# Softmax transposes by VectorE blocks and DRAM, f_j by a DRAM broadcast, two moved gate products and a greater hop in the plan of a four-layer graph network

## The chip, the cores and the metric

The kernel runs on one core of a Trainium2 chip. The metric is the device time in microseconds (us) of one execution. The engines are TensorE (PE), VectorE (DVE), ScalarE (ACT), GpSimd (POOL) and SyncE (SP); here SP issues all the DMAs.

## The reference

There are 128 graphs of 128 nodes with 256 features, and an integer adjacency matrix for each. Four layers follow one another. Each ends with a residual and a normalisation over the features.

```python
# layer 0: four edge scores, chosen by the value of adj
s_k   = leaky_relu(einsum('bid,bjd->bij', x * a_k, x), 0.2)
alpha = softmax(where(adj == k + 1, s_k, NEG_INF))
x = layernorm(x + alpha @ x)
# layer 1: mean of the messages over the incoming edges
msg = einsum('bij,biu->bju', adj, x @ W_msg)
deg = sum(adj, axis=1)
x = layernorm(x + relu(x @ W_upd + msg / max(deg, 1) + bias))
# layer 2: three steps of a gated recurrent unit (GRU)
for i in range(3):
    aggr = einsum('bst,bsd->btd', adj != 0, h @ weight[i])
    h = gru_cell(aggr, h, w_ih, w_hh, b_ih, b_hh)
x = layernorm(x + h)
# layer 3: additive attention
Wh  = x @ W
f_i, f_j = Wh @ a1, Wh @ a2
e   = leaky_relu(f_i[:, :, None] + f_j[:, None, :], 0.2)
alpha = softmax(where(adj > 0, e, NEG_INF))
x = layernorm(x + elu(alpha @ Wh))
```

## The kernel before, in words

Four graphs make a group (G = 4), so that a tile of 128 partitions by 512 columns holds one feature half of a whole group. There are 32 groups (NG = 32). All is float32.

The program is not written in the order in which it runs. The functions `loading`, `layer0`, `layer1`, `gru` and `layer3` only record operations, with their engine, an estimated duration and their dependencies. At the end a planner walks through modelled time. At each step it takes the engine that can start first. Among that engine's operations that are ready by then it takes the one with the least nominal time, and issues it for good. So each engine's order is fixed when the kernel is built, and on the chip an engine runs its list in that order, each instruction as soon as its inputs are there.

The nominal times come from `paced`: a group's GRU fills one period of 91 us, its layer 0 lies two periods to one ahead of that, its layer 1 less than one period ahead, and its layer 3 in the period after. So PE finds products of the layers 0, 1 and 3 of other groups to do while the GRU's chain waits on its other engines. The operations of the GRU are "urgent": on the engines other than PE they go ahead of all others. A result is taken as ready `HOP` (0.3 us) after its producer's end for an urgent consumer, and `SLACK` (1.0 us) after for another. A DMA takes 0.6 us of SP and lands `LANDING` (2.6 us) later.

Three ways of turning and spreading data matter here.

A PE transpose against `ident` goes to a PSUM bank and is copied out by ACT. The function `softmax` does it for the probabilities: four transposes in one bank, then the copy to `probT`. It serves layer 0 and layer 3. In `layer3` PE also spreads f_j, which is column 1 of `wh`, over the partitions: it transposes that column broadcast to 128 columns, and `leaky` reads the result from PSUM into the tile `e`.

The functions `turned` and `back` turn without PE. `DVE.transpose` turns each 32x32 block within its place into a tile `z_...`, one DMA writes it to a DRAM tile `way_...`, and four DMAs fetch the blocks to where they belong. This serves the output of layer 0 (tags 1: z_1, x1T), the output of layer 1 (z_2, h0T) and the new hidden state of each GRU step (z_h, hn). The number of buffers of `z` is 2 where the tile has four blocks of columns (z_2 and z_h), 1 for z_1.

A GRU step's function `step` records the products of the old state with `w_hhT` (`of_h`, in two halves 0 and 1 of the features) and those of the aggregated messages `agT` with `c_gi` (`of_m`), gate by gate: reset R, update Z and candidate C, two halves each. The R and Z gates have PSUM banks of their own (`gate`), the others use `ps`, four banks that all the layers share. `aggregate` multiplies the turned state `hn` by the adjacency, and ACT copies the result to `agT`. `update` makes the new state `hT` on DVE, after which it is turned again.

A float32 product of 128 rows with 512 columns appears as two matmul records in the trace, a PE transpose of 128x128 as one.

Of the kernel before, what the change touches and what calls it, by code (L numbers as in the profile page):

```python
# [17 lines left out]
def kernel(  # L18
# [36 lines left out]
    P = 128  # L55
# [30 lines left out]
    class View:  # L86
# [23 lines left out]
        def to_broadcast(self, shape):  # L110
            return View(self.buf, shape, self.box, self.steps + (("to_broadcast", (shape,), {}),))

        def real(self):
            ap = self.buf.memory()
            for name, a, k in self.steps:
                ap = getattr(ap, name)(*a, **k)
            return ap

    def tile_of(tag, shape, bufs=1, dtype=F32, pool=work):
        buf = Buf(pool, list(shape), dtype, tag, bufs)  # L120
        return View(buf, list(shape), [(0, n) for n in shape])
# [79 lines left out]
                )  # L201


    LANDING = 2.6
    HOP = 0.3
    SLACK = 1.0

    def pe_cost(op, n, sums):
# [151 lines left out]

    def turned(src, n, tag):

        z = tile_of(f"z_{tag}", [P, n, P], 2 if n == 4 else 1)
        DVE.transpose(z, src)
        way = tile_of(f"way_{tag}", [n, P, P], 4, F32, dram)
        SP.dma_start(out=way.rearrange("n p c -> p n c"), in_=z)
        return way
# [31 lines left out]
                res[:, b, :], res[:, b, :], AF.Identity, bias=nmr[:, b : b + 1], scale=rstd[:, b : b + 1]  # L399
            )  # L400

    def softmax(alpha, tag):

        nmax = tile_of(f"nmax_{tag}", [P, G], 2)
        DVE.tensor_reduce(nmax, alpha, AX.X, OP.max, negate=True)
        p = tile_of(f"prob_{tag}", [P, G, N])
        rs = tile_of(f"rsum_{tag}", [P, G], 2)
        for b in range(G):
            ACT.activation(
                p[:, b, :], alpha[:, b, :], AF.Exp, bias=nmax[:, b : b + 1], scale=1.0,  # L410
                accum_out=rs[:, b : b + 1],
            )
        rinv = tile_of(f"rinv_{tag}", [P, G], 2)
        DVE.reciprocal(rinv, rs)
        ps = bank()
        with PE:
            for b in range(G):
                PE.transpose(ps[:, b * N : (b + 1) * N], p[:, b, :], ident)
        pT = tile_of(f"probT_{tag}", [P, G, N])
        ACT.copy(pT, ps.rearrange("p (b n) -> p b n", b=G))  # L420
        return pT, rinv

    def leaky(out, in_, bias):
# [20 lines left out]
    def layer0(g, s):  # L444

        s.a_f = a_f = tile_of("a_f", [P, G, N], 2)
        POOL.tensor_copy(a_f, s.adj)
        alpha = tile_of("alpha0", [P, G, N])
        POOL.memset(alpha, NEG0 / SLOPE)
        xT = []  # L450
        for c in range(KC):
            t = tile_of("xT", [P, T], 3)
            DVE.transpose(t, s.x_blocks[:, c].rearrange("p i f -> p (i f)"))
            xT.append(t)


        def prepared(k):
            mk = tile_of("mk", [P, G, N], 3, U8)
            DVE.tensor_scalar(mk, a_f, float(k + 1), None, op0=OP.is_equal)
            xs = []  # L460
            for c in range(KC):
                t = tile_of("xs", [P, T], 4)
                if c == 0:
                    POOL.tensor_scalar(t, xT[c], acol[:, k, c : c + 1], None, op0=OP.mult)
                else:
                    ACT.mul(t, xT[c], acol[:, k, c : c + 1])
                xs.append(t)
            return mk, xs

        ready = [prepared(0)]  # L470
        for k in range(4):
            if k < 3:
                ready.append(prepared(k + 1))
            mk, xs = ready.pop(0)
            ps = bank()
            with PE:
                PE.needs(mk)
                for b in range(G):
                    cols = slice(b * N, (b + 1) * N)
                    for c in range(KC):  # L480
                        PE.matmul(ps[:, cols], xT[c][:, cols], xs[c][:, cols], start=(c == 0), stop=(c == KC - 1))
            DVE.copy_predicated(alpha.rearrange(FLAT), mk.rearrange(FLAT), ps)

        leaky(alpha, alpha, 0.0)
        pT, rinv = softmax(alpha, "0")
        s.x1 = res = tile_of("xa", [P, G, D], 2)
        for h in range(G // 2):
            ps = bank()
            with PE:
                for j in range(2):  # L490
                    b = 2 * h + j
                    PE.matmul(ps[:, j * D : (j + 1) * D], pT[:, b, :], s.x[:, b, :], start=True, stop=True)
            for j in range(2):
                b = 2 * h + j
                DVE.scalar_tensor_tensor(
                    res[:, b, :], ps[:, j * D : (j + 1) * D], rinv[:, b : b + 1], s.x[:, b, :],
                    op0=OP.mult, op1=OP.add,
                )
        normalise(res, *statistics(res, "0"), "0")
        way = turned(res.rearrange("p b (c n) -> p (b c) n", c=KC), G * KC, "1")  # L500
        s.x1T = tile_of("x1T", [P, G, KC, N])
        back(s.x1T.rearrange("p b c n -> p (b c n)"), way)
# [44 lines left out]
    def gru(g, s):  # L547
# [5 lines left out]
        def step(i, hT, hn):  # L553
# [63 lines left out]
            q1 = hidden(1, terms(C + 1, of_h=both, start=True, stop=True))  # L617
            terms(R, of_h=[1])
            terms(R + 1, of_h=[1])
            terms(Z, of_h=[1])  # L620
            terms(Z + 1, of_h=[1])
            for c in range(KC):
                aggregate(c)
            t0 = reset(0, terms(R, of_m=both, stop=True), q0)
            t1 = reset(1, terms(R + 1, of_m=both, stop=True), q1)
            n0, d0 = candidate(0, terms(C, of_m=both, start=True, stop=True), t0)
# [10 lines left out]
    def layer3(g, s):  # L637


        rT = []  # L640
        for c in range(KC):
            t = tile_of("rT", [P, T], 2)
            POOL.tensor_add(t, s.hT[c], s.h0T[c])
            rT.append(t)
        x3 = tile_of("xc", [P, G, D])
        for c in range(KC):
            cols = slice(c * P, (c + 1) * P)
            DVE.tensor_add(x3[:, :, cols], s.hn[c], s.x2[:, :, cols])
        mv, rstd = statistics(x3, "2")
        wh = tile_of("wh", [P, G, 2 + D])  # L650
        for b in range(G):
            ps = bank()
            with PE:
                for c in range(KC):
                    PE.matmul(
                        ps[:, : 2 + D], rT[c][:, b * N : (b + 1) * N], w3x[:, c, :],
                        start=(c == 0), stop=(c == KC - 1),
                    )
            ACT.mul(wh[:, b, :], ps[:, : 2 + D], rstd[:, b : b + 1])

        ps = bank()
        with PE:
            for b in range(G):
                PE.transpose(
                    ps[:, b * N : (b + 1) * N], wh[:, b, 1:2].to_broadcast([P, N]), ident
                )
        alpha = tile_of("alpha3", [P, G, N])
        POOL.memset(alpha, NEG3)
        e = tile_of("e", [P, G, N])
        for b in range(G):  # L670
            leaky(e[:, b, :], ps[:, b * N : (b + 1) * N], wh[:, b, 0:1])
        DVE.copy_predicated(alpha.rearrange(FLAT), s.m_gt.rearrange(FLAT), e.rearrange(FLAT))
        pT, rinv = softmax(alpha, "3")
        normalise(x3, mv, rstd, "2")

        res = tile_of("xd", [P, G, D], 2)
        neg = tile_of("neg", [P, G, D])
        for h in range(G // 2):
            ps = bank()
            with PE:  # L680
                for j in range(2):
                    b = 2 * h + j
                    PE.matmul(ps[:, j * D : (j + 1) * D], pT[:, b, :], wh[:, b, 2:], start=True, stop=True)
            for j in range(2):
                b = 2 * h + j
                pb = ps[:, j * D : (j + 1) * D]
                DVE.tensor_scalar(
                    neg[:, b, :], pb, rinv[:, b : b + 1], 0.0, op0=OP.mult, op1=OP.min
                )
                ACT.activation(res[:, b, :], pb, AF.Relu, scale=rinv[:, b : b + 1])  # L690
        for h in range(G // 2):
            half = slice(2 * h, 2 * h + 2)
            ACT.activation(neg[:, half], neg[:, half], AF.Exp)
            POOL.tensor_add(res[:, half], res[:, half], x3[:, half])
            DVE.scalar_tensor_tensor(res[:, half], neg[:, half], -1.0, res[:, half], op0=OP.add, op1=OP.add)
        normalise(res, *statistics(res, "3"), "3")
        SP.dma_start(out=out[g * G : (g + 1) * G].rearrange("b n d -> n b d"), in_=res)
# [69 lines left out]
    while left:  # L767
# [24 lines left out]
            buf.free_at = max(buf.free_at, end)  # L792
        for other in op.after.values():
            other.waiting -= 1
            hop = 0.0 if other.engine is e and not op.landing else HOP if other.urgent else SLACK
            other.ready = max(other.ready, end + hop)
            if other.waiting == 0:
                other.engine.ready.append(other)
# [29 lines left out]
```

## Time and profile before

| What | Value |
|---|---|
| Median of 3 runs | 3052.71 us (3050.05 to 3054.14) |
| Profiled execution | 3051.68 us |
| Its span, first to last instruction | 3049.9 us |
| PE busy | 2964.1 us, 97% of the span |
| DVE busy | 1918.7 us, 63% |
| ACT busy | 1234.7 us, 40% |
| POOL busy | 815.4 us, 27% |
| Mean granted PE clock | 0.991 |
| DMA: share of 16 engines, bytes | 35.1%, 232.27 MB |

A busy time is the union of an engine's records, so records that overlap in the pipeline count once. Every operation goes through one recording helper, so all carry the same line (L198) and are told apart by the names of their tiles. The names in the profile lack their numbers: `prob`, `probT` and `alpha` stand for both layer 0 and layer 3. In a row of the groups the columns are count, busy time and mean duration of one (ns), then the idle time of the engine just before, and what ended it. In a timeline row they are start and length in us, the engine, the operation, how many were merged, and in brackets an idle time before it.

### The profile page before, as it was taken

How to read it: one execution, taken by the hardware profiler on the slowest of the kernel's cores; microseconds unless marked ns; L12 is line 12 of the kernel's file. 1: busy time of each engine (PE TensorE's matmuls, PEld its weight loads, DVE VectorE, ACT ScalarE, POOL GpSimd, SP SyncE). 2: the span in 40 equal slices, each digit the busy share in tenths (PEclk: the TensorE clock that was granted, in tenths of full speed). 3: DMA queues.
4: the chain of work that ended last, by engine and by line, in shares of the span. 5: the costliest groups of instructions: out<-in, count | busy, mean ns of one | idle time of the engine just before them, and what ended most of it. 6: DMA issues, size and time to landing. Idle time of an engine off the chain costs nothing.

```text
span 3049.9 us, 33115 instructions
## 1 busy us (share of the span) xinstructions
PE 2964.1 (97%) x10456; PEld 1677.0 (55%) x10456; DVE 1918.7 (63%) x4315; ACT 1234.7 (40%) x2543; POOL 815.4 (27%) x711
## 2 busy tenths in 40 slices
PE   7899999999999999999999999999999999999996
PEld 5455555555555555555555555555555555555543
DVE  5556666566666566666566666666666566665644
ACT  2234444434444434443434444344444344434333
POOL 3222332222222222222223322222322222222222
PEclk9999999999999999999999999999999999999997
DMA  5333333233333333432333432343332344322321
GB/s 133 72 65 86 80 85 76 58 80 85 85 80 66 66 83 83 90 79 60 73 83 80 91 76 58 76 86 82 83 71 59 83 87 87 76 55 50 76 62 42
DMA packets 1034478, 232.27 MB, mean 76 GB/s; under 512 B 817984, under 2 KB 1034176, under 8 KB 1034304
## 3 DMA queue, kind: packets, MB, share of 16 engines
q1 hardware_dynamic: 1034304, 230.16, 35.1%
q8 instruction: 84, 1.38, 0.2%
q14 instruction: 90, 0.74, 0.1%
HBM read 129.38 MB, written 100.66 MB: 75 GB/s over the span
## 4 chain that ended last, share of the span: by engine, by line
PE 91%; DVE 4%; issue 1%; ACT 0%; POOL 0%; SPq 0%; DMA 0%; POOLq 0%; ACTq 0%
PE ps L198 50%; PE gate L198 41%; DVE hT L198 2%; DVE t_d L198 2%; DVE t_r L198 1%; DVE neg L198 0%; SPq L198 0%; ACT xd L198 0%; DVE z L198 0%; DVE xd L198 0%; DMA hn<-way_h 0%; POOL t_d L198 0%; ACT wh L198 0%; DVE st L198 0%; DVE z_h L198 0%
## 5 line engine op out<-in xcount | busy, mean ns | idle before, releaser
L198 PE MATMUL gate<-agT,c_gi 128*128 128x512 f32 x1536 | 711.0, 592 | 0.0
L198 PE MATMUL gate<-hT,w_hhT 128*128 128x512 f32 x1024 | 473.6, 595 | 26.6 <-DVE hT L198 26.6
L198 PEld LDWEIGHTS gate<-agT,c_gi 128*128 128x128 f32 x1536 | 286.8, 190 | 324.3 <-issue 321.0
L198 PE MATMUL ps<-agT,c_gi 128*128 128x512 f32 x768 | 360.7, 592 | 0.0
L198 PEld LDWEIGHTS gate<-hT,w_hhT 128*128 128x128 f32 x1024 | 191.9, 190 | 223.6 <-issue 170.0
L198 POOL TENSOR_TENSOR rstd<-rstd,neg_half 128x4 f32<-128x4 f32 x128 | 141.9, 1109 | 629.2 <-DVE rstd L198 604.8
L198 POOL TENSOR_SCALAR xs<-xT,acol 128x512 f32<-128x512 f32 x128 | 204.0, 1594 | 396.4 <-PE ps L198 389.9
L198 POOL TENSOR_TENSOR t_d<-hT,t_n 128x512 f32<-128x512 f32 x128 | 176.9, 1382 | 471.2 <-ACT t_n L198 467.5
L198 DVE SCALAR_TENSOR_TENSOR t_d<-t_z,t_d 128x512 f32<-128x512 f32 x192 | 196.2, 1022 | 140.6 <-POOL t_d L198 77.7
L198 DVE SCALAR_TENSOR_TENSOR t_r<-t_r,q 128x512 f32<-128x512 f32 x192 | 141.5, 737 | 224.9 <-ACT t_r L198 222.1
L198 ACT ACTIVATE q<-ps,bhn 128x512 f32<-128x512 f32 x192 | 132.0, 688 | 362.9 <-PE ps L198 362.9
L198 PEld LDWEIGHTS ps<-xs,xT 128*128 128x128 f32 x2048 | 243.4, 193 | 17.8 <-issue 15.9
L198 PE MATMUL ps<-xs,xT 128*128 128x128 f32 x2048 | 246.7, 276 | 0.3 <-DVE xb L198 0.3
L198 PE MATMUL ps<-hT,w_hhT 128*128 128x512 f32 x512 | 240.3, 593 | 4.3 <-DVE hT L198 4.3
L198 PE MATMUL ps<-w_um,x1T 128*128 128x512 f32 x512 | 241.5, 595 | 1.6 <-DMA x1T<-way 1.6
L198 ACT ACTIVATE t_n<-t_r,bih 128x512 f32<-128x512 f32 x192 | 138.3, 720 | 245.8 <-DVE t_r L198 245.8
L198 ACT COPY agT<-ps 128x512 f32<-128x512 f32 x192 | 112.5, 586 | 303.0 <-PE ps L198 303.0
L198 PE MATMUL gate<-h0T,w_hhT 128*128 128x512 f32 x512 | 235.0, 592 | 0.0
L198 ACT ACTIVATE t_r<-gate,brz 128x512 f32<-128x512 f32 x192 | 131.9, 687 | 253.5 <-PE gate L198 253.5
L198 PEld LDWEIGHTS ps<-agT,c_gi 128*128 128x128 f32 x768 | 145.7, 190 | 157.4 <-issue 154.0
L198 DVE TENSOR_TENSOR t_r<-t_r,ps 128x512 f32<-128x512 f32 x192 | 131.5, 685 | 145.0 <-PE ps L198 144.9
L198 POOL TENSOR_TENSOR t_d<-h0T,t_n 128x512 f32<-128x512 f32 x64 | 82.1, 1283 | 386.8 <-ACT t_n L198 386.8
(107 smaller groups left out, 4189.5 us busy)
## 6 DMA issues: line engine op xcount, KB each, us to landing
way_h<-z_h SPq DMA_DIRECT2D x192, 256.0 KB, 2.3
hn<-way_h SPq DMA_DIRECT2D x768, 64.0 KB, 2.5
x_blocks<-in_x_dram SPq DMA_DIRECT2D x256, 64.0 KB, 2.4
x_in<-in_x_dram SPq DMA_DIRECT2D x32, 512.0 KB, 4.1
way<-z SPq DMA_DIRECT2D x32, 512.0 KB, 4.3
x1T<-way SPq DMA_DIRECT2D x128, 128.0 KB, 3.0
way<-z SPq DMA_DIRECT2D x64, 256.0 KB, 2.6
h0T<-way SPq DMA_DIRECT2D x256, 64.0 KB, 2.5
```

Of the source, the lines that this page charges most:

```text
L198: getattr(self.engine, name)(*[a.real() if isinstance(a, View) else a for a in args], **{k: a.real() if isinstance(a, View) else a for k, ...
```

## The change

The softmax of layer 0 turns its probabilities with PE for the first group only, the softmax of layer 3 for the last group only. All the others use `turned` and `back` with the new tag p. For all groups but the last, f_j is written as a row per graph to DRAM, and read back with a broadcast to the 128 partitions, into the tile `fj`, on which `leaky` then works in place; the tile `e` is gone. `turned` keeps two buffers only for the tag h, so z_2 and z_p have one. In the GRU step the second halves of the update gates' `of_h` products are recorded behind the aggregates. In the planner, an urgent consumer on PE is taken as ready `PE_HOP` (0.7 us) after its producer.

```diff
+    PE_HOP = 0.7
...
     def turned(src, n, tag):
-        z = tile_of(f"z_{tag}", [P, n, P], 2 if n == 4 else 1)
+        z = tile_of(f"z_{tag}", [P, n, P], 2 if tag == "h" else 1)
...
-    def softmax(alpha, tag):
+    def softmax(alpha, tag, quick):
...
-        ps = bank()
-        with PE:
-            for b in range(G):
-                PE.transpose(ps[:, b * N : (b + 1) * N], p[:, b, :], ident)
         pT = tile_of(f"probT_{tag}", [P, G, N])
-        ACT.copy(pT, ps.rearrange("p (b n) -> p b n", b=G))
+        if quick:
+            ps = bank()
+            with PE:
+                for b in range(G):
+                    PE.transpose(ps[:, b * N : (b + 1) * N], p[:, b, :], ident)
+            ACT.copy(pT.rearrange(FLAT), ps)
+        else:
+            back(pT.rearrange(FLAT), turned(p, G, "p"))
         return pT, rinv
...
-        pT, rinv = softmax(alpha, "0")
+        pT, rinv = softmax(alpha, "0", g == 0)
...
             terms(R + 1, of_h=[1])
+            for c in range(KC):
+                aggregate(c)
             terms(Z, of_h=[1])
             terms(Z + 1, of_h=[1])
-            for c in range(KC):
-                aggregate(c)
...
-        ps = bank()
-        with PE:
-            for b in range(G):
-                PE.transpose(
-                    ps[:, b * N : (b + 1) * N], wh[:, b, 1:2].to_broadcast([P, N]), ident
-                )
+        fj = tile_of("fj", [P, G, N])
+        if g < NG - 1:
+            way = tile_of("way_f", [G, N], 4, F32, dram)
+            SP.dma_start(out=way.rearrange("b n -> n b"), in_=wh[:, :, 1])
+            SP.dma_start(out=fj, in_=way.partition_broadcast(P))
+            rows = [fj[:, b, :] for b in range(G)]
+        else:
+            ps = bank()
+            with PE:
+                for b in range(G):
+                    PE.transpose(ps[:, b * N : (b + 1) * N], wh[:, b, 1:2].to_broadcast([P, N]), ident)
+            rows = [ps[:, b * N : (b + 1) * N] for b in range(G)]
         alpha = tile_of("alpha3", [P, G, N])
         POOL.memset(alpha, NEG3)
-        e = tile_of("e", [P, G, N])
         for b in range(G):
-            leaky(e[:, b, :], ps[:, b * N : (b + 1) * N], wh[:, b, 0:1])
-        DVE.copy_predicated(alpha.rearrange(FLAT), s.m_gt.rearrange(FLAT), e.rearrange(FLAT))
-        pT, rinv = softmax(alpha, "3")
+            leaky(fj[:, b, :], rows[b], wh[:, b, 0:1])
+        DVE.copy_predicated(alpha.rearrange(FLAT), s.m_gt.rearrange(FLAT), fj.rearrange(FLAT))
+        pT, rinv = softmax(alpha, "3", g == NG - 1)
...
-            hop = 0.0 if other.engine is e and not op.landing else HOP if other.urgent else SLACK
+            hop = 0.0 if other.engine is e and not op.landing else SLACK if not other.urgent else HOP
+            if hop == HOP and other.engine is PE:
+                hop = PE_HOP
```

More of the change, by code (lines that the diff above doesn't have):

```diff
@@ L111, in to_broadcast, with partition_broadcast @@
             return View(self.buf, shape, self.box, self.steps + (("to_broadcast", (shape,), {}),))
+        def partition_broadcast(self, n):
+            return View(self.buf, [n, *self.shape], self.box, self.steps + (("partition_broadcast", (n,), {}),))
         def real(self):
```

## The prediction

> **What bounds the kernel now.** I read the busy table first, then the chain that ended last, then a table of two steady stretches, then the waits of TensorE (PE).
>
> ```profile
> PE 2964.1 (97%) x10456; PEld 1677.0 (55%) x10456; DVE 1918.7 (63%) x4315; ACT 1234.7 (40%) x2543; POOL 815.4 (27%) x711
> ...
> PE 91%; DVE 4%; issue 1%; ACT 0%; POOL 0%; SPq 0%; DMA 0%; POOLq 0%; ACTq 0%
> ```
>
> PE is busy for 97% of the span and 91% of the chain is its own; no other engine passes 63%. So the kernel goes as fast as PE gets through its list. The two stretches are one group of graphs each, 92.39 us apart:
>
> ```profile
> 329.19:421.58 92.39, 91.44 (x324) 51.70 (x324) 59.72 (x135) 38.33 (x79) 25.36 (x22) 1.00 0.36 77
> 1530.30:1622.69 92.39, 91.44 (x325) 51.70 (x325) 59.71 (x135) 38.33 (x79) 25.36 (x22) 1.00 0.36 77
> ```
>
> The columns are stretch, length, then busy time of PE, weight loads, DVE, ACT and POOL, the granted clock, DMA share and GB/s. A group costs 91.44 us of PE and 0.95 us of idling; the clock is at full, so it gives nothing more. The waits of PE name that idling:
>
> ```profile
> PE gate L198 <- DVE hT L198: 26.6, 28, 1.0
> ```
>
> 28 times, once per group, a gate product waits for a new hidden state. The timeline at one of them:
>
> ```profile
> 1528.32 1.37 POOL L198 TENSOR_TENSOR t_d<-hT,t_n 128x512 f32<-128x512 f32 x1 [0.32 <-ACT t_n L198]
> ...
> 1528.58 1.66 DVE L198 SCALAR_TENSOR_TENSOR hT<-t_d,t_n 128x512 f32<-128x512 f32 x1
> ...
> 1530.30 3.70 PE L198 MATMUL gate<-hT,w_hhT 128*128 128x512 f32 x8 [0.96 <-DVE hT L198]
> ```
>
> The hT instruction takes 1.66 us beside a POOL instruction; the median of its kind is 0.69. PE waits exactly that 0.97 us of excess. The planner does not know of it (it plans 0.68), and orders this product 0.3 us (HOP) behind hT.
>
> **What the skill says.** (1) The Trainium skill, "SBUF — State Buffer", section "Who interferes with whom": a DVE instruction with two SBUF inputs and a POOL instruction that reads SBUF exclude one another. The trace agrees, with the 1.66 us just shown. (2) "VectorE: DVE Perf Modes", section "The three transpose paths": DVE turns only 32x32 blocks and TensorE a whole 128x128 tile; so the DVE way needs DMAs to move the blocks. The page's 390 ns for TensorE is not the price in this stream; I measure it below at 108 ns. (3) "DMA: Bandwidth & Descriptors", section "Rules for kernel authors": a non-contiguous last dimension becomes one descriptor per element. The f_j write is 512 such elements. The trace has only loads of that kind: acol, 256 elements in 1 KB, 3.4 us to landing; bih, 768 elements, 5.4 us.
>
> **Part 1, TensorE loses 93 transposition sets.** A set is four transposes, one per graph. The softmax of layer 0 keeps them for the first group only, the softmax of layer 3 and f_j for the last only: 3 x 31 = 93 sets go. The groups and the timeline price one:
>
> ```profile
> L198 PE MATMUL ps<-ident,prob 128*128 128x128 f32 x256 | 40.4, 278 | 6.4 <-ACT prob L198 6.4
> ...
> L198 PE MATMUL ps<-ident,wh 128*128 128x128 f32 x128 | 20.2, 279 | 6.1 <-ACT wh L198 6.1
> ...
> 1594.70 1.88 PE L198 MATMUL ps<-hT,w_hhT 128*128 128x512 f32 x4
> 1596.42 0.60 PE L198 MATMUL ps<-ident,wh 128*128 128x128 f32 x4
> 1596.85 0.60 PE L198 MATMUL ps<-hu,a_f 128*128 128x257 f32 x2
> ```
>
> By the groups a set is 40.4/64 = 0.63 us, but that holds the tail that overlaps the next product. From start to start it is 1596.85 - 1596.42 = 0.43 us (0.44 for a prob set at 1610.38). I take 0.43: 93 x 0.43 = **40.0 us off**, of work that is on the path. The waits in front of these sets in the groups (6.4 and 6.1) lie at the ends, where the sets stay.
>
> **Part 2, DVE, ACT, SP and the DMAs in its place.** DVE gains 62 block transposes at the 711 ns of the z_h row: 44 us, from 63% to 64%. ACT loses 62 probT copies (578 ns, 36 us); its leaky now reads SBUF instead of PSUM, bounded by the 256-column rows (SBUF 590 ns, PSUM 471): 0 to 0.12 us x 124 = 0 to 15 us more. ACT stays near 40%. Cost nothing: both lie beside PE, and if that cover went they would cost their 44 and 15 us. SP issues 62 x 5 + 31 x 2 = 372 more DMAs; at the 486 ns of an hn issue this is 181 us, where SP's own waits sum to some 2,100 us. They carry about 40 MB and 178,000 packets on 232 MB and 1,034,000, so the DMA share goes from 35% to some 41%: room enough. The four-buffer limit on PSUM is eased by three banks per group; I count no gain for it.
>
> The latency of both softmaxes grows. Against one set (0.43 us) and one copy stands: DVE 0.7, a write 2.3, four issues 2, landing 2.5, i.e. about 7.5 us; f_j about 4 + 3 = 7 us. In the steady state this has cover: the f_j set of the group at 1596 is used by products at 1615.97 and 1620.27, and these again by nothing on PE, since the output follows. The plan paces layer 0 of a group one to two periods of 91 us ahead of its GRU. First and last group keep the short way. So nothing, with up to 1 us per group if it is wrong.
>
> What is late behind them on SP are the hidden states of the GRU:
>
> ```profile
> way_h<-z_h SPq DMA_DIRECT2D x192, 256.0 KB, 2.3
> hn<-way_h SPq DMA_DIRECT2D x768, 64.0 KB, 2.5
> ...
> acol<-in_L_gnn_a_dram SPq DMA_DIRECT2D x4, 1.0 KB, 3.4
> ...
> 1539.64 2.03 SPq L198 DMA_DIRECT2D hn<-way_h  x4
> ...
> 1546.89 1.06 PE L198 MATMUL ps<-a_ne,hn 128*128 128x128 f32 x8
> ```
>
> These hn loads are issued by 1541.67, land 2.5 us later at 1544.2, and their product starts at 1546.89: 2.7 us to spare. (At 1594.93 it is 1596.83 + 2.5 against 1604.66: 5.3 us.) An SP that stands waiting for the f_j write holds them up. The planner allows this landing 2.6 + 1.0 = 3.6 us; the bounds are 3.4 (acol) and 5.4 (bih), so SP stands 0 to 1.8 us, less than 2.7. I take 0.
>
> **Part 3, z_2 with one buffer.** In layer 1 the second DVE transpose now waits until the first tile has been read by its DMA. It was two buffers. In the steady state layer 1 is ahead of its GRU, and DVE has other work; if the landing (2.6 us median, up to 5.9) is later than planned, DVE stands, with the hT instructions queued behind it and PE behind those: 0 to 0.5 us per group, I take 0. For the first group h0T is late by about 2.6 us with PE in want of work: +2 us, between 0 and 3.
>
> **Part 4, PE_HOP of 0.7 and the two moved products.** Planned readiness isn't waited for on the chip, so the greater hop only alters the order: PE gets 0.4 us more of other work ahead of a product that hangs on hT. Of 0.96 us per group it takes 0.4 at least where the case stays the same, and all of it if a whole filler (0.43 to 1.9 us) slips in; nothing if no filler is ready. Moving the second halves of the two update gates behind the aggregates puts 2 x 0.86 us of PE work between agT's copy (586 ns) and its use, and takes as much from in front of the aggregates; the planner goes by readiness first, so I put it at 0. Waits: 26.6 off at best, 15 on if the new order has more such collisions; I take 60%, **16 us off**.
>
> **Sum.** -40 - 16 + 2 = -54 us. The profiled execution was 3051.68 us (span 3049.9 and 1.8 around it), 1.0 below the median of 3052.71. So a span near 2996 and a median of **2999 us**. A measurement of this kernel tells about 0.2%, 6 us, from no change.
>
> **The rivals.** *A, forecast* (55%): PE's work and most of its waits go, 2983 to 3006. *B, the waits stay or multiply* (31%): every list order has its own collisions of DVE and POOL, and DVE has 44 us more to place. For it: the planner knows nothing of the lock. Against: 0.4 us more margin. With the waits kept 3052.7 - 40 + 2 = 3015; with twice as many 3041. *C, SP's queue delays the GRU* (14%, of which 3% end within 0.2%): hn behind a late f_j (1.8) and four loads of probT (2.1) is late by 3.9 - 2.7 = 1.2 us. Once per group this is 37 us and eats the gain: 3052. Twice per group is 3015 + 74 = **3089, slower**. It decides from 1.3 us of new PE wait per group. For it: SP is in order and the landing of the f_j write is unknown. Against: hn issues have priority in the plan, and the slack is 2.7 to 5.3 us. *D*, the change doesn't act: excluded for the transposes, which are no matter of order; possible for the moved products, and inside A.
>
> **Numbers.** The likeliest is A with 2999. The range starts at the full gain, 3052.7 - 40 - 27 = 2986 less 3 for luck at the ends, and goes to 3035, most of B. Faster 86%, same 3%, slower 11%.
>
> **What would show it.** Right: PE busy near 2924 us with 372 fewer products, a period near 90.5 us, PE waits for hT under 15 us in all, the ident,prob group down to 8 products and ident,wh to 4. Wrong: PE waits for hn, for agT or for probT that come once per group; SP standing on way_f over 2 us; a landing of way_f above 5.4 us; a period above 92.4.

## The result, and the profile after

The changed kernel takes 3173.54 us (median of 4 runs, 3170.81 to 3178.41) against 3051.47 us for the kernel before beside it: a ratio of 1.040, 95% interval 1.038 to 1.042. It is slower by 122 us where 54 us less was forecast. The profiled execution took 3178.41 us with a span of 3176.6.

First the busy table, the chain by engine, and the chain's largest terms by engine and tile:

```profile
PE 2980.7 (94%) x10084; PEld 1673.9 (53%) x10084; DVE 1974.2 (62%) x4377; ACT 1198.8 (38%) x2481; POOL 840.4 (26%) x711
...
PE 78%; DMA 13%; DVE 4%; SPq 2%; issue 1%; ACT 1%; POOL 0%; POOLq 0%; ACTq 0%; DVEq 0%
PE ps L201 41%; PE gate L201 36%; DMA way_h<-z_h 10%; DMA hn<-way_h 2%; SPq L201 2%; DVE hT L201 1%; DVE t_d L201 1%; DVE z_h L201 1%; ACT t_z L201 1%; DVE xb L201 0%; DVE t_r L201 0%; DMA x1T<-way 0%; DMA q<-in_L_gnn_w_hh_dram 0%; DVE mk L201 0%; ACT xd L201 0%
```

Two things are to be seen. PE runs 372 transposes fewer and is yet busy for 16.6 us longer. And DMA, 0% of the chain before, is now 13%, nearly all of it one transfer: `way_h<-z_h`, the write of the GRU's new hidden state. PE's waits say what that costs (total, times, longest):

```profile
PE ps L201 <- DMA hn<-way_h: 129.9, 32, 5.2
...
PE gate L201 <- DVE hT L201: 3.5, 4, 2.2
```

The once-per-group wait for hT is gone, and a once-per-group wait for hn stands in its place, four times as long. The span books balance: PE's waits sum to 182.7 us against 72.5 (+110), PE busy to 2980.7 against 2964.1 (+17), and the span has grown by 126.7.

One such place, from the timelines of SP and of PE (SPq is SP issuing DMAs):

```profile
1558.36 0.38 SPq L201 DMA_DIRECT2D way_f<-wh  x1
...
1560.03 0.38 SPq L201 DMA_DIRECT2D way_h<-z_h  x1
...
1570.31 1.91 SPq L201 DMA_DIRECT2D hn<-way_h  x4
1572.32 0.43 SPq L201 DMA_DIRECT2D fj<-way_f  x1
...
1574.29 2.04 PE L201 MATMUL ps<-a_ne,hn 128*128 128x128 f32 x8 [3.91 <-DMA hn<-way_h]
```

The new f_j write goes out 1.67 us ahead of a hidden state. SP then issues nothing for 10 us. It doesn't stand waiting for f_j, whose read-back comes after the hn loads; it waits for `way_h` to land. The transfers by name give that f_j write's usual landing, and the answer for this one way_h its own, as min/median/max:

```profile
way_f<-wh SPq DMA_DIRECT2D x31, 2.0 KB, 10.6
```

```profile
DMA to landing us min/median/max: 10.3/10.3/10.3
```

2 KB take 10.6 us, and the 256 KB behind them 10.3 us, where a hidden state's write otherwise takes 2.4. The DMA engines are not overloaded meanwhile: from 1562 to 1568 us, with both writes under way, their mean busy share is 0.02. The stretches around this wait (length, then busy time of PE, weight loads, DVE, ACT, POOL; granted PE clock, DMA share, GB/s):

```profile
1570.40:1574.29 3.89, 0.00 (x0) 0.03 (x1) 1.12 (x2) 0.00 (x0) 1.50 (x1) 0.99 0.60 103
1574.29:1576.50 2.21, 2.21 (x9) 2.18 (x10) 0.00 (x0) 0.16 (x1) 0.00 (x0) 0.50 0.96 165
1576.50:1580.00 3.50, 3.50 (x9) 1.60 (x8) 1.77 (x5) 3.34 (x8) 0.61 (x1) 0.84 0.54 86
1580.00:1584.00 4.00, 4.00 (x11) 1.78 (x10) 3.21 (x7) 2.80 (x10) 0.10 (x1) 1.00 0.25 66
```

After the wait PE is granted half its clock. The 0.84 is a mean over the change back: up to 1577.59 it is 0.50, from 1577.60 on 1.00, so the half clock lasts 3.3 us. That is why fewer products took longer.

### The profile page after: what moved, and what is told of

The parts are those of the page before. It is cut to its first block, busy times and chain, and to the rows that moved or that the text cites. A ratio compares the mean times of both kernels' runs of the same rounds, so it can differ in the third digit from the quotient of the medians.

```text
span 3176.6 us, 32922 instructions
## 1 busy us (share of the span) xinstructions
PE 2980.7 (94%) x10084; PEld 1673.9 (53%) x10084; DVE 1974.2 (62%) x4377; ACT 1198.8 (38%) x2481; POOL 840.4 (26%) x711
## 3 DMA queue, kind: packets, MB, share of 16 engines
q1 hardware_dynamic: 1218816, 270.88, 41.8%
## 4 chain that ended last, share of the span: by engine, by line
PE 78%; DMA 13%; DVE 4%; SPq 2%; issue 1%; ACT 1%; POOL 0%; POOLq 0%; ACTq 0%; DVEq 0%
PE ps L201 41%; PE gate L201 36%; DMA way_h<-z_h 10%; DMA hn<-way_h 2%; SPq L201 2%; DVE hT L201 1%; DVE t_d L201 1%; DVE z_h L201 1%; ACT t_z L201 1%; DVE xb L201 0%; DVE t_r L201 0%; DMA x1T<-way 0%; DMA q<-in_L_gnn_w_hh_dram 0%; DVE mk L201 0%; ACT xd L201 0%
## 5 line engine op out<-in xcount | busy, mean ns | idle before, releaser
L201 PE MATMUL gate<-hT,w_hhT 128*128 128x512 f32 x1024 | 515.5, 630 | 3.5 <-DVE hT L201 3.5
L201 PEld LDWEIGHTS gate<-agT,c_gi 128*128 128x128 f32 x1536 | 293.4, 191 | 329.3 <-issue 316.5
L201 POOL TENSOR_SCALAR xs<-xT,acol 128x512 f32<-128x512 f32 x128 | 223.6, 1750 | 480.3 <-PE ps L201 395.2
L201 PEld LDWEIGHTS gate<-hT,w_hhT 128*128 128x128 f32 x1024 | 198.8, 205 | 170.9 <-issue 157.5
L201 PE MATMUL ps<-a_ne,hn 128*128 128x128 f32 x1024 | 156.5, 302 | 130.1 <-DMA hn<-way_h 129.9
L201 POOL TENSOR_TENSOR t_d<-hT,t_n 128x512 f32<-128x512 f32 x128 | 186.9, 1460 | 287.6 <-ACT t_n L201 287.6
L201 PE MATMUL ps<-w_um,x1T 128*128 128x512 f32 x512 | 233.5, 598 | 11.1 <-DMA x1T<-way 11.1
L201 PEld LDWEIGHTS ps<-a_ne,hn 128*128 128x128 f32 x1024 | 147.8, 213 | 169.6 <-issue 158.4
L201 DVE SCALAR_TENSOR_TENSOR t_d<-t_z,t_d 128x512 f32<-128x512 f32 x192 | 132.6, 691 | 146.5 <-ACT t_z L201 145.7
```

The source lines that it names most:

```text
L201: getattr(self.engine, name)(*[a.real() if isinstance(a, View) else a for a in args], **{k: a.real() if isinstance(a, View) else a for k, ...
```

## The experiments

Theory W: the element-wise f_j write holds up the hidden state's write, and this is all the loss. Its rivals: S, SP has too many DMAs to issue and comes to the hn loads too late; O, the new order (hop and moved products) puts the hn products too early. Medians are followed by the ratio to the kernel before on the same chip.

**fj_on_pe.** The change, with f_j left on PE for all groups:

```diff
-        if g < NG - 1:
+        if False:
             way = tile_of("way_f", [G, N], 4, F32, dram)
```

> All of the change but f_j, which PE spreads for every group as before (62 transposition sets go instead of 93). Theory W (the write of f_j in 512 elements of 4 bytes holds up the write of the hidden state that is issued next on the same queue, and that alone costs the time): PE waits for hn fall from 129.9 us to under 10, the largest landing of way_h from 10.7 us to about 5, and the median is 3052 - 62 x 0.43 = 3025 less what the greater hop saves (0 to 26 us): 2998 to 3030. Theory S (SP, with 310 more issues for the softmaxes, reaches the hn loads too late): waits for hn stay above 60 us, median above 3090. Theory O (the order made by the hop and the moved products puts the hn products too early): the same, waits for hn stay, median above 3090.

Measured: 2987.57 us, 0.979 (0.978 to 0.981). No wait for hn is left among PE's waits, the largest landing of way_h is 4.4 us, and PE busy is 2927.5. That is below W's range of 2998 to 3030, since the waits for hT went entirely and each had cost PE more than its idling (below). It keeps the 310 DMAs of the softmaxes, the hop and the moved products, so S and O fall: f_j through DRAM alone turns a gain of 2% into a loss of 4%.

**fj_dram_only.** The kernel before, with f_j alone through DRAM: `partition_broadcast`, and the block from `fj = tile_of(...)` to the predicated copy as in the change.

> The kernel before, with only f_j going through DRAM for the groups 0 to 30. Theory W: way_f lands after about 10 us, and wherever a hidden state is written behind it PE waits; with one such wait of 4 us and some 1.5 us of lower clock per group the median is 3052 - 13 + 31 x 5.5 = about 3210, in any case above 3080 if a way_h follows within 10 us. Theories S and O: 31 x 2 more issues and no new hop, so no new wait: 3052 - 13 = about 3039.

Measured: 3094.77 us, 1.015 (1.014 to 1.017). PE's waits:

```profile
PE ps L201 <- DMA hn<-way_h: 36.9, 18, 3.1
PE gate L201 <- DVE hT L201: 29.0, 28, 1.4
```

Alone, and with the old hop and order, the f_j write makes the same wait, so W holds against S and O again. It does so in every second group only, and for 2 us instead of 4: in this order the write goes out some 0.5 us behind a way_h, and it is the hn loads issued after it that come late (those issued from 1899.73 us on take 6.0 to 7.3 us to land, where 2.4 is their median). What such a write costs depends on what follows it on the DMAs. The 3210 us of the expectation took one wait of 4 us in every group, as the whole change has it.

**probe_writes.** The kernel before, with one write per group that nothing reads, in four forms by turns:

```diff
+        kind = g % 4
+        if kind == 0:
+            pw = tile_of("pw_elem", [G, N], 4, F32, dram)
+            SP.dma_start(out=pw.rearrange("b n -> n b"), in_=wh[:, :, 1])
+        elif kind == 1:
+            pw = tile_of("pw_apart", [G, N, 128], 4, F32, dram)
+            SP.dma_start(out=pw[:, :, 0].rearrange("b n -> n b"), in_=wh[:, :, 1])
...
+            DVE.tensor_copy(pk, wh[:, :, 1])
+            pw = tile_of("pw_sixteen", [N, G], 4, F32, dram)
+            SP.dma_start(out=pw, in_=pk)
+        else:
...
+            pw = tile_of("pw_packed", [G, N], 4, F32, dram)
+            SP.dma_start(out=pw.rearrange("b n -> n b"), in_=pk)
```

> The kernel before with one more write to DRAM per group, which nothing reads, in four forms by turns (8 groups each): pw_elem, as f_j is written now (512 elements of 4 bytes, neighbours in DRAM come from different partitions); pw_apart, the same elements 512 bytes apart in DRAM; pw_packed, the same places as pw_elem from a packed 128x4 tile; pw_sixteen, 128 pieces of 16 bytes. Theory W by the number of pieces: elem, apart and packed all land after about 10 us, sixteen after about 2.5. If the clash of writes to the same stretch of DRAM is the cause: apart lands in under 5 us, elem and packed after 10. If reading elements with a step from SBUF is the cause: packed lands in under 4 us, elem and apart after 10.

Measured, from the transfers by name (count, size, median us to landing):

```profile
pw_elem<-wh SPq DMA_DIRECT2D x8, 2.0 KB, 10.1
pw_apart<-wh SPq DMA_DIRECT2D x8, 2.0 KB, 2.3
pw_sixteen<-pk SPq DMA_DIRECT2D x8, 2.0 KB, 1.9
pw_packed<-pk SPq DMA_DIRECT2D x8, 2.0 KB, 9.4
```

The number of pieces alone is not the cause: the same 512 elements, 512 bytes apart, land in 2.3 us. Nor is reading them with a step: packed, they still take 9.4. What costs is that 512 neighbouring 4-byte elements are written to one stretch of DRAM as separate pieces.

**probe_steps.** How near is near? The same with the elements 8, 16, 64 and 256 bytes apart:

```diff
+        gap = (2, 4, 16, 64)[g % 4]
+        pw = tile_of(f"pw_step{4 * gap}", [G, N, gap], 2, F32, dram)
+        SP.dma_start(out=pw[:, :, 0].rearrange("b n -> n b"), in_=wh[:, :, 1])
```

> The kernel before with one more write per group of 512 elements of 4 bytes that nothing reads, 8, 16, 64 or 256 bytes apart in DRAM by turns (8 groups each). At 4 bytes apart it landed after 10.1 us, at 512 bytes apart after 2.3. If elements clash within 32 or 64 bytes: 64 and 256 land in under 3.5 us, 8 and 16 after 5 to 10. If they clash within 512 bytes: all four land after more than 4 us, less the further apart. If only whole neighbours matter: 8 lands fast already.

Measured on the writes of the groups 0 to 3, in this order of distance (min/median/max of the one):

```profile
DMA to landing us min/median/max: 5.2/5.2/5.2
DMA to landing us min/median/max: 3.2/3.2/3.2
DMA to landing us min/median/max: 2.3/2.3/2.3
DMA to landing us min/median/max: 2.2/2.2/2.2
```

The medians of eight each are 4.8, 3.2, 2.2 and 2.2 us. With 10.1 us for 4 bytes apart, landing falls as fewer elements share 64 bytes (16, 8, 4, then one), and from 64 bytes on nothing more is to be had. The clash lies within a stretch larger than 16 and up to 64 bytes. Nearness alone isn't all of it either: the pieces of pw_sixteen also lie four to 64 bytes, but there are only 128 of them, and they land in 1.9 us. The runs show neither how number and nearness act together nor why such writes take so long.

**fj_act_queue.** The change, with the f_j write issued by ACT:

```diff
-            SP.dma_start(out=way.rearrange("b n -> n b"), in_=wh[:, :, 1])
+            ACT.dma_start(out=way.rearrange("b n -> n b"), in_=wh[:, :, 1])
```

> The whole change, with the element-wise write of f_j issued by ACT on its own queue instead of SP's. Theory Q (the write of the hidden state stands behind it in SP's queue, in order): the landing of way_f stays near 10 us, the largest landing of way_h falls to about 5 us, waits of PE for hn under 20 us, median 2980 to 3010. Theory R (it blocks what all queues share): way_h written within 10 us after it still lands after 8 to 10 us, median above 3100 if a way_h follows so closely in the new order.

Measured: 3100.57 us, 1.016 (1.015 to 1.018). The largest landing of way_h is still 9.8 us, and here is one, issued on SP's queue 1.7 us after ACT issued the f_j write (8.6 us to landing):

```profile
1612.43 0.38 SPq L201 DMA_DIRECT2D way_h<-z_h  x1
1619.34 0.34 SPq L201 DMA_DIRECT2D fj<-way_f  x1
1622.12 1.91 SPq L201 DMA_DIRECT2D hn<-way_h  x4
```

Its own landing answer is 9.7 us. So R holds: another queue doesn't pass the write. PE's waits for hn fell to 34.6 us and the time by 73, with 38.8 us of PE's waits put down to agT instead; the plan's order differs, so this is no measure of what the queue is worth. The waits for agT are a second way by which the slow landing reaches PE. In the group just shown ACT stands 5.94 us for `fj`, up to 1624.62, with the copy to agT next in its list; the copy starts at 1625.80, though its product ended at 1622.78, and PE waits 3.59 us for it. In the changed kernel too ACT stands still for `fj`, 227.5 us in all, in fj_packed 2.4.

**fj_packed.** The change, with f_j packed and written in pieces of 16 bytes:

```diff
-        fj = tile_of("fj", [P, G, N])
+        fj = tile_of("fj", [P, N, G])
         if g < NG - 1:
-            way = tile_of("way_f", [G, N], 4, F32, dram)
-            SP.dma_start(out=way.rearrange("b n -> n b"), in_=wh[:, :, 1])
+            fcol = tile_of("fcol", [P, G], 2)
+            DVE.tensor_copy(fcol, wh[:, :, 1])
+            way = tile_of("way_f", [N, G], 4, F32, dram)
+            SP.dma_start(out=way, in_=fcol)
             SP.dma_start(out=fj, in_=way.partition_broadcast(P))
-            rows = [fj[:, b, :] for b in range(G)]
+            rows = [fj[:, :, b] for b in range(G)]
...
-            leaky(fj[:, b, :], rows[b], wh[:, b, 0:1])
+            leaky(fj[:, :, b], rows[b], wh[:, b, 0:1])
-        DVE.copy_predicated(alpha.rearrange(FLAT), s.m_gt.rearrange(FLAT), fj.rearrange(FLAT))
+        DVE.copy_predicated(alpha, s.m_gt, fj.rearrange("p n b -> p b n"))
```

> The whole change, but f_j is first packed by DVE into 4 neighbouring elements per partition (128x4), written to DRAM as 128 pieces of 16 bytes in node order, and read back in that order; leaky and the predicated copy then read it with a step of 4. Theory W with the number of small pieces as its cause: landing of way_f 2.3 to 3.5 us instead of 10.6, waits of PE for hn under 15 us, median 2985 to 3010. If the cause were the use of DRAM for f_j at all, or SP's order, or the hop: landing or waits stay, median above 3100.

Measured: **2978.18 us**, 0.976 (0.975 to 0.978): it beats both kernels, by 72 and 195 us. Its busy table, its f_j transfers, and a stretch of 2,400 us from its middle:

```profile
PE 2913.4 (98%) x10084; PEld 1638.9 (55%) x10084; DVE 1942.4 (65%) x4408; ACT 1221.9 (41%) x2481; POOL 841.4 (28%) x711
```

```profile
fj<-way_f SPq DMA_DIRECT2D x31, 256.0 KB, 3.5
...
way_f<-fcol SPq DMA_DIRECT2D x31, 2.0 KB, 2.2
```

```profile
300.00:2700.00 2400.00, 2400.00 (x8327) 1348.18 (x8326) 1617.57 (x3667) 1012.33 (x2052) 703.69 (x589) 1.00 0.45 94
```

PE never stands still there, at full clock. The products are those of the changed kernel, so the 67.3 us by which that one's PE is busy for longer (2980.7) come with its waits, most of them by the slow clock after each.

**hop_only, move_only, softmax_only.** The other parts, each alone on the kernel before.

```diff
+    PE_HOP = 0.7
...
+            if hop == HOP and other.engine is PE:
+                hop = PE_HOP
```

> The kernel before with PE_HOP alone. By the prediction's part 4 the waits of PE for hT (26.6 us) go by 60% or all: median 3050 - 16 to - 26 = 3024 to 3034. Rival: the collision of DVE and POOL that makes the wait is not planned, so the new order has its own: waits stay, 3045 to 3055.

Measured: 3028.88 us, 0.992 (0.991 to 0.994). The waits for hT fall from 26.6 to nothing in the steady state (3.6 us in all, at the end); 6.9 us of waits for probT come in their place, 29 times. The forecast's term was right.

```diff
+            for c in range(KC):
+                aggregate(c)
             terms(Z, of_h=[1])
             terms(Z + 1, of_h=[1])
-            for c in range(KC):
-                aggregate(c)
```

> The kernel before with the two update gate products recorded behind the aggregates, nothing else. Prediction's part 4: 0, so 3044 to 3056. Rival: the aggregates come 1.7 us earlier in PE's order, meet hn loads that have not landed, and PE waits up to 1.7 us in each step: up to 3050 + 31 x 3 x 1.7 = 3208; or the order gets the agT copies covered and the hT waits fall: down to 3024.

Measured: 3051.06 us, 0.9998 (0.9989 to 1.0006), with 26.3 us of waits for hT as before: no change, as forecast.

```diff
-        pT, rinv = softmax(alpha, "0")
+        pT, rinv = softmax(alpha, "0", g == 0)
...
-        pT, rinv = softmax(alpha, "3")
+        pT, rinv = softmax(alpha, "3", g == NG - 1)
```

> The kernel before with only the two softmaxes turned through DVE and DRAM (and z_2 with one buffer), old hop, old order of recording. By the price of a set 62 x 0.43 = 27 us off, waits for hT as the new order makes them (0 to 54 us against 26.6): 3050 - 27 = 3023, between 2997 and 3050. If the 310 more DMAs stood in the way of the hidden states: waits for hn above 30 us and a median above 3050.

(`softmax` and `turned` as in the change.) Measured: 2987.55 us, 0.979 (0.977 to 0.980), better than the expected range and the same as fj_on_pe, which has the hop and the moved products besides. In this order PE has no steady wait for hT even with the old hop. So the two gains don't add up: each takes away the same waits.

**fj_packed_hop03.** The packed kernel with `PE_HOP = 0.3`.

> The kernel with packed f_j (2978 us) with PE_HOP at 0.3, the old value. If the greater hop is what took the waits for hT away: they come back, about 26 us, median 2995 to 3008. If the order of this kernel has no such collision anyway: 2975 to 2985.

Measured: 2982.12 us, 0.977 (0.975 to 0.979), against 2978.18 for 0.7: the hop is worth 4 us at most where the order has no such collision, and not 26. A group takes 89.86 us against 89.85 (measured as below), so the 4 us lie at the ends.

**fj_packed_quick2.** The packed kernel with PE transposes in layer 0 for the groups 0 and 1 (`softmax(alpha, "0", g <= 1)`).

> The kernel with packed f_j, with PE transposes in the softmax of layer 0 for the second group too. In the packed kernel PE waits 10.4 us for x1T of the first group near 63 us, where the kernel before used that time for the second group's transposes and products (1.6 us of wait for x1T). If this fills the gap: one set more (0.43 us) and up to 5 us of waiting less, median 2973 to 2978. If the first group's chain is what ends last there: 2978 to 2981, no change.

Measured: 2978.05 us, 0.976 (0.974 to 0.978). The first wait for x1T shrank from 10.4 to 1.4 us and the time stayed: at the start the first group's chain ends last, and the wait was only where the slack showed.

## Why the prediction was wrong, point by point

**What bounds the kernel: right.** With PE's work reduced and nothing new in its way, the time follows PE: fj_packed.

**Part 1, the sets: right.** A period (the time of one group) is taken here between the starts of the same product, the first on h0T, 24 groups apart: before 451.09 and 2668.52, so 92.39 us. From fj_on_pe to fj_packed one set per group goes, with PE full in both, and the period falls from 90.29 us (447.84, 2614.80) to 89.85 (448.00, 2604.43). So a set is worth 0.44 us, as forecast; 93 are 41 us where 40 stood.

**Part 2, the load on the other engines: right, f_j's latency apart.** DVE 62%, ACT 38%, DMA share 41.8% (41 forecast), 184,513 packets more (178,000). The longer way of the softmaxes costs nothing, as softmax_only shows. f_j's way was put at 7 us; in the group shown above it is 18 us from the issue of its write (1558.36) to its first use (1576.34).

**Part 2, the landing of the f_j write: this step failed.** It was bounded by 3.4 and 5.4 us, from the loads acol and bih, and measured 10.6. Loads of single elements were the wrong nearest row for a write of neighbouring elements; the upper end should have stayed open, and nothing else in the trace of before had that form. The second half of the step failed too: I priced it as SP standing in wait for f_j, with 2.7 us of slack. What comes late is the next large write itself, which the f_j write holds up on the DMAs. That is rival C's place, hn behind f_j, with another mechanism and another price.

**Rival C's price.** 1.2 us per collision was worked out; it is 4.2 us of waiting (129.9 over 31 groups) and 2.2 us by which PE is busy for longer (67.3 over 31), most of it the clock: 3.3 us at half clock are 1.65 us lost. The period says nearly the same: 96.13 us (466.46, 2773.48) against 89.85 of fj_packed, 6.3 in every group. The lower clock stood in none of the prediction's cases. The Trainium skill, "TensorE: Matmul & The Clock Gate", section "Part 1: The HAM clock gate (the "warmup" mystery)", has it: after an idle window of about 3.4 us PE gets 4 of 8 clock pulses. The trace agrees in part, with 0.50 after 3.91 us and 1.00 after the 0.96 us waits of the kernel before. But 0.50 also follows a wait of 2.09 us (fj_dram_only, at 1908.63), and 1.00 a wait of 3.48 us (the changed kernel, at 1862.76). The changed kernel's 30 other waits for hn of over 3.6 us are all followed by 0.50; of the 14 that fj_dram_only has up to 2,700 us, 1.8 to 3.1 us long, 7 are. So the length of a wait doesn't settle it alone.

**Part 3, z_2 with one buffer:** forecast +2 us at the start. fj_packed_quick2 shows that the waits at the start moved without changing the time; the one buffer by itself was not tried.

**Part 4, hop and moved products:** forecast -16 and 0; alone they measured -22 and 0. The wait for hT was priced too low, at its 0.96 us of idling: from before to fj_on_pe the period falls by 2.10 us, which leaves 1.23 for the wait beside two sets of 0.44. The trace of before agrees: from the start of the four transposes ahead of that wait, at 1528.73, to the product behind it, at 1530.30, it is 1.57 us, where 0.44 is usual, and that product's first record takes 0.70 us where 0.59 is usual: 1.13 and 0.11 us more. In the whole change the softmaxes' new order takes these waits away already, and the hop adds nothing to it.

**The sum.** By group, from 92.39 us: -1.3 for the three sets and -1.2 for the wait for hT give the 89.85 of fj_packed; +6.3 for the f_j write gives 96.13. Over 31 groups that is 116 of the 122 us; the rest lies at the start and the end.

## What to carry to other kernels

Don't write hundreds of single small elements side by side into DRAM from different partitions: pack them (pieces of 16 bytes were enough here), or put them 64 bytes apart. Price an unknown transfer by a row with the same direction and the same neighbourhood, and leave its upper end open when there is none; then ask which transfer is issued next, on any queue. Price a wait of PE with its clock: waits of about 4 us cost half as much again here, and half of those of about 2 us were followed by the slow clock too.

## What the runs showed of the hardware that I had not expected

A 2 KB write to DRAM takes 10.1 us to land where its 512 elements are neighbours, 4.8, 3.2 and 2.2 us where they are 8, 16 and 64 bytes apart, and 1.9 us in pieces of 16 bytes. For that time a 256 KB write issued after it doesn't land either (10.3 us instead of 2.4), also from another engine's queue (9.7).
